# Turning the last state of a gated graph network by DMA instead of by TensorE, with the attention layer one period later

## The chip, the cores and the metric

The kernel runs on one core of a Trainium2 chip. The core has five engines that work through their own instruction queues in order: TensorE (PE, matrix products and transposes), VectorE (DVE), ScalarE (ACT), GpSimd (POOL) and SyncE (SP, which here only issues transfers). Sixteen DMA engines move data. The metric is device time in microseconds (us) of one execution; less is better.

## The reference, cut to what matters

There are 64 graphs of 256 nodes with 256 features each. Two layers follow each other, each on a normalized input and added to `x`:

```python
# layer 0: three steps of a gated graph network
h = jnp.maximum(_layernorm(x, axis=-1), 0.0)
A = (adj != 0).astype(x.dtype)
for i in range(3):
    m = jnp.einsum('bnd,de->bne', h, weight[i])
    aggr = jnp.einsum('bst,bsd->btd', A, m)
    h = _gru_cell(aggr, h, w_ih, w_hh, b_ih, b_hh)   # gates r, z, n from aggr and h; h = (1-z)*n + z*h
x = x + h
# layer 1: graph attention with 4 heads of 64 features
h = jnp.maximum(_layernorm(x, axis=-1), 0.0)
h = (h @ W.T + b).reshape(Bb, Nn, Hh, Cc)
l_src = jnp.einsum('bihc,hc->bih', h, a_src)
l_dst = jnp.einsum('bjhc,hc->bjh', h, a_dst)
logits = jax.nn.leaky_relu(l_src[:, :, None, :] + l_dst[:, None, :, :], ALPHA)
logits = jnp.where(adj_matrix[..., None] == 1, logits, NEG_INF)
probs = jax.nn.softmax(logits, axis=2)
x = x + jnp.einsum('bijh,bjhc->bihc', probs, h).reshape(Bb, Nn, Hh * Cc)
```

## The kernel before, in words

**Tiling.** Two graphs are worked on together, a "pair"; there are 32 pairs, 0 to 31. A tile "by nodes" has nodes on the 128 partitions (`x`, `xn`, `hNhi`, `hNlo`); a tile "by features" has features there (`hT_a`, the state of layer 0; `hT_b`, the normalized input of layer 1). Gates want the state by features, the aggregation over edges and the residual want it by nodes, so the state is turned after each of the three steps.

**The written-out order.** Nothing is scheduled by a tool. `at(tick, phase, p, fn)` puts a piece of work into a plan, and at the end all pieces are emitted tick by tick, in a tick first phase STEP, then READY, then REST, within a phase the later pair first. This one order fixes the queue of every engine. A step of layer 0 takes 6 ticks (`tick_0` to `tick_5`), a pair has its three steps at ticks 0, 12 and 24 after its own start `t0`, and `t0` is 18 ticks after the one of the pair before; so two pairs alternate every 6 ticks, and the order repeats every 18 ticks, called a period here. A tick named alone is counted from a pair's `t0`; "tick 13 of the period" is the same modulo 18.

**Layer 0.** Of a step the later sections name these instructions: `tick_0` builds `pa`, the aggregation (L470), from `hNhi` and `hNlo`; `tick_1` ends with the VectorE sums `T<-aggr,hT_a` and `T<-T,hT_a` (L491, L492); `tick_3` has `pe<-pd,m` on VectorE (L510), which reads the bank `pd` before `tick_4` adds the product `pd<-T,w_h` to it; `tick_4` and `tick_5` have `pn` on VectorE (L526) and TensorE; `new_n` has `R` on GpSimd (L541); `update` writes the new state into `hT_a` (L557 to L559).

**Turning.** `back(l, i)` turns the state of graph `i` by four TensorE transposes into the bank `pback` (L808). After steps 0 and 1 ScalarE and VectorE split it into `hNhi` and `hNlo` for the next aggregation (L798, L799); after step 2 `residual` adds it to `x` on VectorE (L814), at ticks 31 and 32. There are two other ways to turn in the kernel. `plan_turn` does it by way of DRAM: VectorE splits the 32-bit words into 16-bit halves (`halve`, tile `words`, L387), SP stores them (L389), a transposing transfer brings them back (`turn`, tile `turned`, L393), and VectorE puts the halves together (`join`, L399). It serves the normalized inputs, `hT_a` of pairs from 2 on and `hT_b` of pairs up to 28. `plan_relu_T` does it with eight TensorE transposes and two ScalarE instructions for the other pairs (L372, L373).

**Layer 1** of a pair runs between steps of later pairs: normalization at ticks 32 to 34, `values` (`pv`, L864), the score rows by way of DRAM, head maxima (`any`, L949), two accumulating transfers from POOL (L930) that add rows to the logits, `leaky` and `exps` on ScalarE (L969, L984), and `output`: products `po` (L573), `rden` and `o` on VectorE (L582, L584), the addition to `x` on GpSimd (L589), and the store (L562). The adjacency is loaded twice (L115): once for `edge` (L764), once for `noedge` (L838, function `bar`), which is also turned by a transposing transfer into `link` (L916). The last three pairs end in an order of their own (`plan_tail`).

**Buffers.** A tag has as many buffers as `BUFS` says, otherwise one. Tags that the change touches: `x` (5), `adj` (2), `xn` (2), `words` (1), `turned` (1), `hT_a` (2).

## Time and profile before

| | |
|---|---|
| median of 3 runs | 2498.57 us (2495.76 to 2505.38) |
| profiled execution, its own time | 2498.09 us |
| its span, first to last instruction | 2496.3 us |
| granted TensorE clock | 0.997 |
| PE, PEld busy | 99%, 88% |
| DVE, ACT, POOL busy | 80%, 58%, 20% |
| DMA: software queue (POOL), hardware queue (SP) | 27.4%, 27.0% of 16 engines |
| moved | 313.72 MB, mean 126 GB/s |

The page is of one profiled execution. PE is TensorE's products, PEld its weight loads, which overlap them. Products are pipelined: each is shown from its start to its end, and the next starts before that end. The chain of waits follows the work that ended last back to the start. A group of instructions is one line of the kernel with its tiles, with its busy time, the mean duration of one, and the idle time of the engine just before it. The timeline lists one engine's instructions by start (in us from the span's start) and duration; idle time before an instruction stands in brackets, with what ended it.

### The profile page before, as it was taken

The page shows a single profiled execution, that of the slowest core. Times are in us where ns is not written, and L with a number is a line of the kernel's source. Part 1 is how long each engine was busy: PE and PEld are TensorE (multiplying, and loading weights), DVE is VectorE, ACT ScalarE, POOL GpSimd, SP SyncE. Part 2 cuts the span into 40 slices and gives each one's busy share as a digit, 9 for nine tenths or more (in the row PEclk, how much of TensorE's full clock was granted, in tenths as well). Part 3 has the DMA queues.
Part 4 walks back from the last instruction along what each step waited for, and adds up shares of the span by engine and source line. Part 5 has one row for each costly group of instructions (what it writes and reads, how often), then busy time and mean ns, then how long its engine had stood idle before and what let it go on. Part 6 is the DMA issues. An engine that isn't in the chain of part 4 may idle for free.

```text
span 2496.3 us, 37566 instructions
## 1 busy us (share of the span) xinstructions
PE 2464.2 (99%) x13446; PEld 2191.9 (88%) x13446; DVE 1992.2 (80%) x4671; ACT 1437.5 (58%) x3007; POOL 494.3 (20%) x419
## 2 busy tenths in 40 slices
PE   8999999999999999999999999999999999999998
PEld 6888888888988888988888988888888889888887
DVE  5678877888877888777888778888778888778767
ACT  3445556555556555566565566565565555665664
POOL 0011121221221121212121212121212222212212
PEclk9999999999999999999999999999999999999999
DMA  3025656455656456656556565556565556564455
GB/s 95 9 68 119 152 119 153 121 127 134 136 127 155 119 126 143 132 131 147 116 131 148 117 146 138 116 130 147 122 153 127 123 132 140 125 157 118 107 109 110
DMA packets 322090, 313.72 MB, mean 126 GB/s; under 512 B 166560, under 2 KB 282224, under 8 KB 321904
## 3 DMA queue, kind: packets, MB, share of 16 engines
q0 software_dynamic: 33728, 130.03, 27.4%
q1 hardware_dynamic: 286608, 181.29, 27.0%
q8 instruction: 106, 1.74, 0.3%
q14 instruction: 80, 0.66, 0.1%
q10 hardware_dynamic: 1568, 0.01, 0.0%
HBM read 215.62 MB, written 56.60 MB: 109 GB/s over the span
## 4 chain that ended last, share of the span: by engine, by line
PE 83%; DVE 12%; ACT 3%; issue 1%; DMA 1%; POOL 0%; SPq 0%; ACTq 0%; DVEq 0%; POOLq 0%
PE pd L313 18%; PE pn L313 13%; PE pc L313 9%; PE po L573 8%; PE pe L313 7%; PE pa L470 5%; PE qb L448 5%; PE p L313 5%; PE pv L864 5%; PE qa L448 4%; PE pback L808 2%; DVE hT_a L559 2%; DVE any L949 2%; DVE R L558 2%; DVE hNlo L799 1%
## 5 line engine op out<-in xcount | busy, mean ns | idle before, releaser
L313 PE MATMUL pn<-aggr,w_a 128*128 128x256 f32 x1536 | 364.9, 380 | 2.8 <-DVE pn L526 2.8
L313 PE MATMUL pd<-T,w_a 128*128 128x256 f32 x1536 | 366.4, 382 | 0.0
L541 POOL TENSOR_TENSOR R<-hT_a,hn 128x512 f32<-128x512 f32 x96 | 141.9, 1479 | 1124.5 <-ACT hn L537 1042.5
L313 PEld LDWEIGHTS pn<-aggr,w_a 128*128 128x128 f32 x1536 | 286.9, 190 | 44.3 <-DVE pn L526 2.1
L313 PEld LDWEIGHTS pd<-T,w_a 128*128 128x128 f32 x1536 | 288.1, 191 | 37.6
L573 PEld LDWEIGHTS po<-val,zz 128*128 128x128 f32 x2048 | 244.9, 192 | 4.5
L537 ACT ACTIVATE hn<-pn,bi 128x256 f32<-128x256 f32 x384 | 160.4, 470 | 145.6 <-PE pn L313 145.4
L589 POOL TENSOR_TENSOR x<-x,o 128x256 f32<-128x256 f32 x124 | 137.1, 1107 | 538.3 <-DVE o L584 538.3
L558 DVE SCALAR_TENSOR_TENSOR R<-Z,R 128x512 f32<-128x512 f32 x192 | 132.5, 690 | 137.9 <-POOL R L541 126.3
L573 PE MATMUL po<-val,zz 128*128 128x65 f32 x2048 | 242.1, 272 | 0.0
L969 ACT ACTIVATE zz<-zz,val 128x256 f32<-128x256 f32 x496 | 223.7, 505 | 0.0
L949 DVE CUSTOM_DVE_ANT_0 any<-drow,noedge 128x256 f32<-128x256 f32 x496 | 209.1, 422 | 9.3 <-DMA drow<-score_dram 0.5
L455 ACT ACTIVATE R<-pc,brz 128x256 f32<-128x256 f32 x192 | 80.5, 470 | 230.8 <-PE pc L313 230.8
L526 DVE SCALAR_TENSOR_TENSOR pn<-R,hn 128x512 f32<-128x512 f32 x192 | 149.1, 777 | 77.3 <-ACT R L455 54.7
L455 ACT ACTIVATE R<-pe,brz 128x256 f32<-128x256 f32 x192 | 80.4, 470 | 213.5 <-PE pe L313 213.5
L313 PE MATMUL pd<-T,w_h 128*128 128x256 f32 x768 | 184.4, 383 | 3.1 <-DVE pe L510 0.4
L313 PE MATMUL pc<-aggr,w_a 128*128 128x256 f32 x768 | 182.5, 381 | 0.0
L313 PE MATMUL p<-T,w_a 128*128 128x256 f32 x768 | 181.9, 379 | 0.6 <-DVE w_a L247 0.6
L313 PE MATMUL pe<-aggr,w_a 128*128 128x256 f32 x768 | 181.4, 379 | 0.0
L313 PE MATMUL pc<-hT_a,w_h 128*128 128x256 f32 x768 | 181.4, 379 | 0.0
L799 DVE TENSOR_TENSOR hNlo<-pback,hNhi 128x512 fp32r<-128x512 f32 x128 | 88.2, 689 | 110.9 <-ACT hNhi L798 110.9
L313 PEld LDWEIGHTS pd<-T,w_h 128*128 128x128 f32 x768 | 143.5, 190 | 32.8 <-DVE pe L510 14.5
(183 smaller groups left out, 5323.0 us busy)
## 6 DMA issues: line engine op xcount, KB each, us to landing
zz<-score_dram POOLq DMA_DIRECT2D x62, 1024.0 KB, 11.0
zz<-topT_dram POOLq DMA_DIRECT2D x62, 1024.0 KB, 7.9
adj<-in_adj_dram SPq DMA_DIRECT2D x64, 512.0 KB
drow<-score_dram SPq DMA_DIRECT2D x62, 512.0 KB
x<-in_x_dram SPq DMA_DIRECT2D x32, 512.0 KB
out_dram<-x SPq DMA_DIRECT2D x31, 512.0 KB
words_dram_a<-words_a SPq DMA_DIRECT2D x30, 512.0 KB
words_dram_b<-words_b SPq DMA_DIRECT2D x29, 512.0 KB
```

What stands on the lines that cost most here:

```text
L313: nc.tensor.matmul(pt[:, ts(c, N)], w[:, k, j * D + c * P : j * D + (c + 1) * P], src[:, k, :], start=start and c == 0 and k == 0, stop=(c ...
L448: nc.tensor.matmul(pt, w_n[:, j, :], src, start=start, stop=True, skip_group_check=True)
L455: nc.scalar.activation(of(dst, i)[:, c, :], src[:, c, :], AF.Tanh, bias=brz[:, g0 + c : g0 + c + 1], scale=0.5)
L470: nc.tensor.matmul(pt[:, ts(i, N)], hN[half][:, i * KN + s, ts(e, P)], edge[:, i * KN + s, :], start=(s == 0 and half == 0), stop=(s == KN ...
L526: nc.vector.scalar_tensor_tensor(by_c(self.bank(f"pn{i}")), of(self.R, i), 1.0, of(self.hn, i), op0=ALU.add, op1=ALU.mult)
L537: nc.scalar.activation(n__[:, c, :], p_n[:, c, :], AF.Tanh, bias=bi[:, 2 * KD + c : 2 * KD + c + 1])
L541: nc.gpsimd.tensor_sub(of(self.R, i), of(self.hT(), i), n__)
L558: nc.vector.scalar_tensor_tensor(d_, of(self.Z, i), 1.0, d_, op0=ALU.add, op1=ALU.mult)
L573: nc.tensor.matmul(po[:, ts(h_, VC)], zz[:, j, h_, ts(s, P)], v["val"][:, i * KN + j, ts(h_, VC)], start=(j == 0), stop=(j == KN - 1),)
L589: add(v["x"][:, r, :], v["x"][:, r, :], o)
L949: nc.vector.tensor_tensor_reduce(any_, drow[r // KN][:, h, :], v["noedge"][:, r, :], 1.0, -3.0e38, ALU.add, ALU.max, accum_out=v["top"][:, ...
L969: nc.scalar.activation(zz[:, h, :], zz[:, h, :], AF.Prelu, alpha=ALPHA, bias=v["val"][:, r, S0 + H + h : S0 + H + h + 1],)
```

## The change

For pairs 0 to 21 ("home") the state after the third step is turned by `plan_turn`: halved at tick 31, turned at tick 33, joined at tick 37 into a buffer of tag `xn`, and then added to `x` by an accumulating transfer from POOL at tick 38. The TensorE transposes and the two additions on VectorE of that step are not emitted for them. Layer 1 of a pair starts `S` ticks later: 18 for home pairs, 15, 12, 9, 6 and 3 for pairs 22 to 26, and 0 from pair 27 on. Pairs 22 to 26 turn their normalized input with `plan_relu_T` instead of `plan_turn`. `adj` has one buffer instead of two, and its two loads and the making of `noedge` are moved (first load to tick -5; second load to tick 40 for home pairs and `bar` to tick 46, from 22 and 35); `x` has six buffers instead of five. The second turning transfer of home pairs (`turned_b`) is issued at tick 37 + 18 instead of 35, and `link` at 38 + 18 instead of 37. `plan_turn` is written for any shape of blocks.

```diff
--- before.py
+++ after.py
@@ -99,7 +99,7 @@
         return ps_m.tile([P, 512], F32, tag="mm", name=name)
 
     BUFS = {
-        "x": 5, "adj": 2, "edge": 2, "noedge": 2, "hT_a": 2, "xn": 2, "val": 2, "row": 2, "zz": 4, "o": 2,
+        "x": 6, "adj": 1, "edge": 2, "noedge": 2, "hT_a": 2, "xn": 2, "val": 2, "row": 2, "zz": 4, "o": 2,
     }
 
     def buf(tag, shape, name, dtype=F32):
@@ -377,27 +377,30 @@
             at(t, REST, p, fn(k))
         return w
 
-    def plan_turn(src, tag, name, p, ticks):
+    def plan_turn(src, dst, name, p, ticks):
+
 
 
         w = {}
 
         def halve():
-            words = buf("words", [P, R, 2, D], f"words_{name}", U16)
-            nc.vector.tensor_copy(words, src().bitcast(U16).rearrange("q r (d w) -> q r w d", w=2))
-            w["rows"] = dram.tile([R, P, 2 * D], U16, tag="words", name=f"words_dram_{name}")
-            nc.sync.dma_start(w["rows"].rearrange("r q e -> q r e"), words.rearrange("q r w d -> q r (w d)"))
+            y = src()
+            nb, n = y.shape[1:]
+            words = buf("words", [P, nb, 2, n], f"words_{name}", U16)
+            nc.vector.tensor_copy(words, y.bitcast(U16).rearrange("q b (n w) -> q b w n", w=2))
+            w["rows"] = dram.tile([nb, P, 2 * n], U16, tag="words", name=f"words_dram_{name}")
+            nc.sync.dma_start(w["rows"].rearrange("b q e -> q b e"), words.rearrange("q b w n -> q b (w n)"))
 
         def turn():
-            w["turned"] = buf("turned", [P, 2, KD * T], f"turned_{name}", U16)
-            nc.sync.dma_start_transpose(
-                w["turned"].rearrange("q w (k n) -> q (w k) n", k=KD), w["rows"].rearrange("r q e -> (r q) e")
-            )
+            nb, _, n2 = w["rows"].shape
+            w["turned"] = buf("turned", [P, n2 // P, nb * P], f"turned_{name}", U16)
+            nc.sync.dma_start_transpose(w["turned"], w["rows"].rearrange("b q e -> (b q) e"))
 
         def join():
-            w["hT"] = buf(tag, [P, KD, T], f"hT_{name}")
+            w["hT"] = dst()
             nc.vector.tensor_copy(
-                flat(w["hT"]).bitcast(U16).rearrange("q (n w) -> q n w", w=2), w["turned"].rearrange("q w n -> q n w")
+                flat(w["hT"]).bitcast(U16).rearrange("q (n w) -> q n w", w=2),
+                flat(w["turned"]).rearrange("q (w n) -> q n w", w=2),
             )
 
         at(ticks[0], READY, p, halve)
@@ -757,7 +760,8 @@
         if p == 0:
             v["x"], v["adj"] = first
         else:
-            rest(-16, lambda: v.update(x=load_x(p), adj=load_adj(p, "adj")))
+            rest(-16, lambda: v.update(x=load_x(p)))
+            rest(-5, lambda: v.update(adj=load_adj(p, "adj")))
 
         def to_edge():
             v["edge"] = buf("edge", [P, R, N], f"edge_{p}", F32R)
@@ -770,7 +774,9 @@
         ready(-1 if p else -2.5, to_edge)
         if dma_a:
             ready(-9.5, lambda: nc.scalar.activation(flat(xn_a["xn"]), flat(xn_a["xn"]), AF.Relu))
-            h = plan_turn(lambda: xn_a["xn"], "hT_a", f"a{p}", p, [t0 - 9, t0 - 8, t0 - 3])
+            h = plan_turn(
+                lambda: xn_a["xn"], lambda: buf("hT_a", [P, KD, T], f"hT_a{p}"), f"a{p}", p, [t0 - 9, t0 - 8, t0 - 3]
+            )
         else:
             h = plan_relu_T(xn_a, "hT_a", f"a{p}", p, [t0 - 4, t0 - 3])
 
@@ -812,6 +818,16 @@
         def residual(i):
             xi = flat(v["x"][:, i * KN : (i + 1) * KN, :])
             nc.vector.tensor_add(xi, v["pback", i], xi)
+
+
+
+        S = max(0, min(3 * SUB, 3 * (NPAIR - 5 - p)))
+        home = S == 3 * SUB
+        if home:
+            h_3 = plan_turn(
+                lambda: h["hT"], lambda: buf("xn", [P, R, D], f"h_{p}"), f"h{p}", p, [t0 + 31, t0 + 33, t0 + 37]
+            )
+            rest(38, lambda: nc.gpsimd.dma_start(flat(v["x"]), flat(h_3["hT"]), accum_op=ALU.add))
 
         for l in range(L):
             end = last and l == L - 1
@@ -826,7 +842,8 @@
                 ready(t + SUB, lambda g=g: g.update(0))
                 ready(t + SUB, lambda g=g: g.update(1))
                 for i in range(PB):
-                    rest(t + SUB + 1 + i, back(l, i))
+                    if not (home and l == L - 1):
+                        rest(t + SUB + 1 + i, back(l, i))
 
 
         def load_adj_1():
@@ -840,19 +857,23 @@
                 v["noedge_rows"] = dram.tile([R, P, N], BF16, tag="noedge", name=f"noedge_dram_{p}")
                 nc.sync.dma_start(v["noedge_rows"].rearrange("r q t -> q r t"), v["noedge"])
 
-        rest(16 if last else 22, load_adj_1)
-        ready(28 if last else 35, bar)
+
+        rest(16 if last else 22 + S if S > 12 else 36 if S >= SUB else 22, load_adj_1)
+        ready(28 + S if S > 12 else 40 if S >= SUB else 30 if S else 28, bar)
         if last:
             plan_tail(t0, p, v, g, lambda i: turn_back(L - 1, i), residual)
             return
 
-        dma_b = p < NPAIR - 3
-        later = SUB if dma_b else 0
-        xn_b = plan_norm(lambda: v["x"], f"b{p}", p, [t0 + 32, t0 + 33, t0 + 33, t0 + 34], dma_b)
+        dma_b = S in (0, 3 * SUB) and p < NPAIR - 3
+        later = SUB + S if p < NPAIR - 3 else 0
+        xn_b = plan_norm(lambda: v["x"], f"b{p}", p, [t0 + S + t for t in (32, 33, 33, 34)], dma_b)
         if dma_b:
-            hb = plan_turn(lambda: xn_b["xn"], "hT_b", f"b{p}", p, [t0 + 34.1, t0 + 35, t0 + 41])
+            hb = plan_turn(
+                lambda: xn_b["xn"], lambda: buf("hT_b", [P, KD, T], f"hT_b{p}"), f"b{p}", p,
+                [t0 + S + t for t in (34.1, 37 if home else 35, 41)],
+            )
         else:
-            hb = plan_relu_T(xn_b, "hT_b", f"b{p}", p, [t0 + 35, t0 + 36])
+            hb = plan_relu_T(xn_b, "hT_b", f"b{p}", p, [t0 + S + 35, t0 + S + 36])
 
         def values(r0):
             def fn():
@@ -932,7 +953,7 @@
                 )
             return fn
 
-        rest(37 if dma_b else 36, linked)
+        rest(38 + S if home else 37 + S if p < NPAIR - 3 else 36, linked)
         ready(38 + later, barred_in(0, 0))
         ready(39 + later, barred_in(0, 1))
         ready(40 + later, barred_in(1, 0))

```

## The prediction

> **What bounds the kernel now.** I read the page's engine row first, then the groups, then the transposes by their tile name, and then one period in order of time, engine by engine. First the page:

> ```profile
> PE 2464.2 (99%) x13446; PEld 2191.9 (88%) x13446; DVE 1992.2 (80%) x4671; ACT 1437.5 (58%) x3007; POOL 494.3 (20%) x419
> ...
> PE 83%; DVE 12%; ACT 3%; issue 1%; DMA 1%; POOL 0%; SPq 0%; ACTq 0%; DVEq 0%; POOLq 0%
> ...
> L313 PEld LDWEIGHTS pd<-T,w_h 128*128 128x128 f32 x768 | 143.5, 190 | 32.8 <-DVE pe L510 14.5
> ```

> TensorE is the bound: 99% busy, 83% of the last chain. It runs from product to product, so what counts is the distance between starts. First `pa` products 18 ticks apart lie 75.48 us apart in nearly every period from tick 78 to tick 546. The third line is the one regular hole: `pd<-T,w_h` waits for VectorE's `pe` (L510). The work to be removed, by its tile:

> ```profile
> L808 PE MATMUL pback<-ident,hT_a x768: 272/273/417, 52.4 to 2454.0; 128*128 128x128 f32 x192
> ...
> L814 DVE TENSOR_TENSOR x<-pback,x x64: 658/687/692, 138.5 to 2455.0; 128x512 f32<-128x512 f32 x64
> ```

> Now one period in order of time (start, duration, then the instruction; brackets are idle time before it). VectorE's queue:

> ```profile
> 1275.06 0.18 DVE L582 RECIPROCAL rden<-po 128x4 f32<-128x4 f32 x1 [0.39 <-PE po L573]
> ...
> 1280.91 0.68 DVE L838 TENSOR_SCALAR noedge<-adj 128x1024 bf16<-128x1024 int32 x1
> ...
> 1282.32 0.18 DVE L582 RECIPROCAL rden<-po 128x4 f32<-128x4 f32 x1
> ...
> 1288.61 0.69 DVE L492 TENSOR_TENSOR T<-T,hT_a 128x512 f32<-128x512 f32 x1
> ...
> 1293.52 0.69 DVE L799 TENSOR_TENSOR hNlo<-pback,hNhi 128x512 fp32r<-128x512 f32 x1 [0.54 <-ACT hNhi L798]
> 1294.13 0.69 DVE L510 TENSOR_TENSOR pe<-pd,m 128x512 f32<-128x512 f32 x1
> ```

> and TensorE's:

> ```profile
> 1258.75 0.60 PE L808 MATMUL pback<-ident,hT_a 128*128 128x128 f32 x4
> 1259.19 1.89 PE L313 MATMUL p<-T,w_a 128*128 128x256 f32 x8
> ...
> 1280.10 1.90 PE L573 MATMUL po<-val,zz 128*128 128x65 f32 x16
> ...
> 1294.17 0.59 PE L448 MATMUL qb<-T4n,w_n 128*128 128x256 f32 x2
> 1294.87 1.99 PE L313 MATMUL pd<-T,w_h 128*128 128x256 f32 x8
> ```

> Four transposes take 0.44 us of TensorE's order (1258.75 to 1259.19), though each shows 0.273. `qb` pairs elsewhere are followed 0.43 later, so `pd` could start at 1294.60 and starts at 1294.87: a hole of 0.27 us. VectorE has one idle gap of 0.39 between 1262.5 and 1293, and reaches the `rden` at 1282.32 only 0.3 after its `po` ended (1282.00). From there to `pe` it has no slack of its own: the 0.54 before `hNlo` comes round by ScalarE from VectorE's own `hn`.

> [...] here f32 transposes go by every 0.109 us. [...] a 1 MB accumulate lands in a median 11.0 us beside other transfers, 7.9 elsewhere.

> **The change part by part**, against the profiled execution (2498.09 us, span 2496.3, 1.8 around it; 0.5 below the median 2498.57).

> *Transposes removed.* S is 18 for pairs 0 to 21 ("home"): 22 x 8 x 0.109 = -19.2 us on the bound engine.

> *Transposes added.* Pairs 22 to 26 (S = 15, 12, 9, 6, 3) turn the normalized x on TensorE again: 5 x 8 x 0.109 = +4.4. Net -14.8.

> *VectorE, ticks 13 to 17.* Two residual adds go (0.60 of its queue each), `words_h` comes (1.14, the rate of `words_a`, 1243.30 to 1244.43). It stands before the wait for `qb` at 1261.98, where VectorE idled 1.30: hidden. Without that cover it costs 0.5 a period.

> *noedge* goes from tick 17 to tick 10, into a stretch idle 3.1 us at 1249.9: free there. At tick 17 it frees 0.60 of queue, but only 0.3 counts, as `rden` then waits for `po`.

> *join of h* (1.15, as `hT_a` at 1266.61 to 1267.76) comes right after `T<-T,hT_a` at 1288.61, in the stretch without slack. From `po`'s end: `rden` 0.03 later, 11.81 from `rden` to `pe` as shown (1282.32 to 1294.13), +1.15, and 0.74 from `pe`'s start to `pd`'s: 13.73. TensorE needs 1294.60 - 1282.00 = 12.60. The hole becomes 1.13, +0.86. It needs the head maxima beside it, which start with tick 67 of pair 0; so joins of pairs 2 to 21: 20 x 0.86 = +17.2. Bounds: 0 if something else absorbs it, 1.15 + 0.3 a period if the freed 0.3 doesn't come: 0 to +24.

> *Periods without a join.* The 0.27 hole is seen 29 times; it stays inside the 20 above, and the nine others lose it at most: -2.4.

> *Catch-up.* Layer 1 of pairs 22 to 27 follows at 15 ticks instead of 18. Counting queue times, VectorE holds 22 to 26 us for each six ticks there, against 24 to 28 for TensorE; the regular worst six ticks hold 29.4 against 25.7 and pass with 0.27. But xn of S = 3 and the statistics of S = 6 fall in ticks 1 to 4, without slack. I take 3; bounds 0 and +20 (4 for each of five pairs).

> *Layer 1 a period later*: the same products later; ticks 24 to 42, without layer 1, already run at 64.3 us for 18, its work. Nothing.

> *Transfers.* Each home pair adds a store, a transpose and an accumulate of 512 KB, on SP, SP and POOL. SP now has `words_h` store, adj load and `turned_h` behind `turned_a`; DMA is idle from 1267 to 1277 and the join comes at 1289: hidden. `turned_b` then waits for the join (the one `turned` buffer), and out of turn behind it in SP's queue stand x, link and adj. The old places of those:

> ```profile
> 1206.62 3.16 SPq L393 DMA_TRANSPOSE turned_b<-words_dram_b  x1
> ...
> 1213.43 0.39 SPq L120 DMA_DIRECT2D x<-in_x_dram  x1
> ```

> After: join over at 1214.7 on this period's clock, `turned_b` issued in 2 to 3 us, x at 1217 to 1218. Its data, with the accumulate interleaved, is through at 1221.5 to 1224. `st_a` reads x at 1222.26, then 0.9 later than that because of the hole; `pn` behind it waits for ScalarE anyway and is due on TensorE at 1226.5: lateness up to some 1.8 us costs nothing. Link (read from tick 8), adj (tick 10) and `hT_b` (1225.89) have 5 us or more. POOL waits for the join too; behind it stands `R` at 1226.37, after an idle 17.6. The sixth x buffer keeps the reuse distance of before; the one adj buffer alternates with 3 ticks or more to spare. Free.

> Sum: -19.2 + 4.4 + 17.2 - 2.4 + 3 = +3.0; 2498.1 + 3.0 = **2501 us**.

> **Rivals.** *The join is absorbed.* Then -14.8 and the holes as before or gone: 2481 to 2486. For it: 1.3 and 3.1 us idle elsewhere on VectorE; against: none between 1282 and 1293. *The late x.* If x lands later than 1.8 us after `st_a` wants it, every further microsecond is one of TensorE, 20 times: at +1.5 us that is +30, with the sum 2531. It decides from a landing at about 1225. For it: SP's queue is in order and the transpose's issue takes up to 3.4 us; against: four microseconds of idle DMA from 1220. *Catch-up in VectorE's tight ticks*, 3 to 4 us for each of five pairs: 2513 to 2518. *The transfers are only hidden work* and the hole is 0.5 instead of 0.86: 2494.

> **How the numbers follow.** Cancelling, with smaller and larger holes: 0.53 (2488 to 2510). Join absorbed: 0.13. Late x: 0.15. Catch-up: 0.19. A change under 0.5% (12.5 us) can't be told from none here. Faster 0.13 (the absorbed join alone), slower 0.34 (the late x and the catch-up), same 0.53. The range leaves out the fastest absorbed cases and the late x from 1.2 us on: 2484 to 2524.

> **What would show it.** `pback` down to 592; a hole of about 1.1 us before `pd<-T,w_h` once a period, laid to `pe`, in the periods from tick 72 to 430; the period there still 75.5 us; the two before it under 65. A period of 74.6 says the join is absorbed. A wait of `st_a` for x, or of `hT_b` for `turned_b`, says transfers are late. Periods over 80 between ticks 440 and 545 say catch-up. I am wrong if VectorE's queue in ticks 17 to 21 has a slack that this one period hides, or if DMA beside the accumulate is slower than these windows.

## The result and the profile after

The changed kernel takes 2530.8 us (median of 4 runs, 2523.8 to 2532.3); the kernel before took 2502.0 on the same chip at the same time. The ratio is 1.0112, with a 95% interval of 1.0081 to 1.0144: slower, by about 28 us. The forecast was 2501 with a range up to 2524. The profiled execution is the quickest of the four: 2523.8 us, span 2522.0, 25.7 above the span of before.

First the page of the kernel after: the engine row, the row of the last chain, and two groups of products (busy us, mean ns of one, then the idle time just before them and what ended it).

```profile
PE 2455.3 (97%) x13310; PEld 2182.0 (87%) x13310; DVE 2012.7 (80%) x4661; ACT 1442.4 (57%) x3017; POOL 514.1 (20%) x441
...
PE 80%; DVE 14%; ACT 3%; DMA 2%; issue 1%; POOL 0%; SPq 0%; DVEq 0%; POOLq 0%; ACTq 0%
...
L313 PE MATMUL pn<-aggr,w_a 128*128 128x256 f32 x1536 | 367.8, 383 | 13.0 <-DVE pn L529 13.0
...
L313 PE MATMUL pd<-T,w_h 128*128 128x256 f32 x768 | 184.1, 383 | 22.3 <-DVE pe L513 22.3
```

TensorE has less to do (2455 us busy, 2464 before) and yet ends later: it is idle. Two groups wait: `pd<-T,w_h` for `pe`, as forecast (3.1 before), and `pn<-aggr,w_a` for `pn` on VectorE, which was not forecast (2.8 before).

The transposes by tile name, and the regular period in order of time: VectorE's queue first, then TensorE's (start, duration, instruction, idle time before it in brackets).

```profile
L814 PE MATMUL pback<-ident,hT_a x592: 272/273/328, 52.3 to 2479.0; 128*128 128x128 f32 x198
```

```profile
1273.69 0.69 DVE L495 TENSOR_TENSOR T<-T,hT_a 128x512 f32<-128x512 f32 x1
1274.29 1.22 DVE L401 COPY h<-turned_h 128x2048 uint16<-128x2048 uint16 x1
...
1280.34 0.69 DVE L513 TENSOR_TENSOR pe<-pd,m 128x512 f32<-128x512 f32 x1
```

```profile
1279.54 0.59 PE L451 MATMUL qb<-T4n,w_n 128*128 128x256 f32 x2
1281.08 1.99 PE L313 MATMUL pd<-T,w_h 128*128 128x256 f32 x8 [0.95 <-DVE pe L513]
```

`pback` fell from 768 to 592, which is 22 x 8 fewer. The join of h stands where it was expected, and `pd` starts 1281.08 - 1279.54 - 0.43 = 1.11 us after it could: the forecast was 1.13. So the regular period is as forecast, 75.45 us against 75.48. The time went elsewhere. The stretch view of the kernel after, one row for each stretch of 18 ticks: the first is a regular period, the others start at ticks 420, 438, 456, 474, 492, 510 and 528. Columns: stretch, length, busy time (and instructions) of PE, PEld, DVE, ACT and POOL, granted clock (the share of full speed that TensorE got), DMA share, GB/s.

```profile
762.00:837.45 75.45, 74.50 (x407) 66.57 (x405) 62.86 (x145) 44.41 (x94) 17.05 (x16) 1.00 0.76 154
1742.88:1818.13 75.25, 75.25 (x415) 67.34 (x413) 61.83 (x145) 44.52 (x94) 15.91 (x14) 1.00 0.57 134
1818.13:1898.31 80.18, 79.96 (x438) 71.22 (x437) 62.33 (x148) 47.41 (x99) 16.88 (x15) 1.00 0.50 116
1898.31:1980.17 81.86, 77.09 (x423) 67.65 (x422) 63.19 (x149) 49.23 (x102) 12.39 (x11) 1.00 0.50 123
1980.17:2064.03 83.86, 79.18 (x427) 69.58 (x425) 65.60 (x162) 47.57 (x99) 22.46 (x20) 0.98 0.64 135
2064.03:2143.74 79.71, 78.64 (x442) 70.26 (x441) 61.07 (x153) 48.56 (x99) 15.05 (x13) 1.00 0.71 119
2143.74:2231.68 87.94, 84.41 (x462) 75.18 (x461) 66.55 (x163) 49.28 (x101) 19.64 (x16) 0.96 0.63 140
2231.68:2311.37 79.69, 76.00 (x416) 67.03 (x414) 63.28 (x151) 45.59 (x96) 15.71 (x14) 1.00 0.57 133
```

The six periods from tick 438 on are the catch-up, in which layer 1 comes back from 18 ticks late to none. They take 493.2 us. The work that belongs there comes to 468.3: six periods as before (6 x 75.48 = 452.9), 4.4 for the added transposes, and 11.0 for the layer 1 of one pair that was put off from the start. (A period without layer 1 takes 63.37 us at its steadiest, one with it and without a hole 74.37, as `e7_join_43` below shows.) **The catch-up thus loses 24.9 us**, where the forecast had 3, and that is nearly the whole difference in this execution. The granted clock is below 1 in two of the six.

What such a loss is made of, in the kernel after at 1916 to 1923 us. Three queues in order of time: VectorE, GpSimd, TensorE.

```profile
1916.19 0.69 DVE L529 SCALAR_TENSOR_TENSOR pn<-R,hn 128x512 f32<-128x512 f32 x1
1916.80 0.68 DVE L523 TENSOR_TENSOR Z<-pd,m 128x512 f32<-128x512 f32 x1
1917.80 2.06 DVE L353 TENSOR_SCALAR xn_b<-x,mv_b,rstd_b 128x256 f32<-128x256 f32 x4 [0.33 <-POOL rstd_b L348]
...
1920.24 1.55 DVE L970 CUSTOM_DVE_ANT_0 any<-drow,noedge 128x256 f32<-128x256 f32 x1
...
1921.72 0.69 DVE L529 SCALAR_TENSOR_TENSOR pn<-R,hn 128x512 f32<-128x512 f32 x1
```

```profile
1917.74 1.23 POOL L951 DMA_DIRECT2D zz<-topT_dram  x1
1918.50 1.70 POOL L951 DMA_DIRECT2D zz<-score_dram  x1
1920.02 1.48 POOL L544 TENSOR_TENSOR R<-hT_a,hn 128x512 f32<-128x512 f32 x1
```

```profile
1917.03 1.97 PE L313 MATMUL pn<-aggr,w_a 128*128 128x256 f32 x8 [0.65 <-DVE pn L529]
1918.83 1.89 PE L313 MATMUL pd<-T,w_a 128*128 128x256 f32 x8
1922.47 1.99 PE L313 MATMUL pn<-aggr,w_a 128*128 128x256 f32 x8 [1.74 <-DVE pn L529]
```

TensorE has only `pd` between its two `pn` products. In that time VectorE makes the normalized input of layer 1 (`xn_b`) and head maxima (`any`), the second of which takes 1.55 us beside GpSimd's `R` instead of the usual 0.42. VectorE works in order (its second `pn` starts at 1921.72, just as `any` ends), so this `pn` comes late and TensorE stands (1.74 us). (This `pn` reads the half of `R` that ScalarE made by 1917.3; GpSimd's `R` is the other graph's, so it is not what `pn` waits for.) Such a stretched `any` stands five times in this trace: of 512, five take 0.95 to 1.55 us, and each of these starts while GpSimd's `R` (four times) or `x<-x,o` (once) runs and ends 0.28 to 0.29 us after it, here at 1921.79 against 1921.50. The other 507 take 0.39 to 0.43 us. Why `any` is held up is not shown.

### The profile page after: what moved, and what is told of

It reads as the page before. It is cut to its first block, busy times and chain, and to the rows that moved or that the text cites. A ratio compares the mean times of both kernels' runs of the same rounds, so it can differ in the third digit from the quotient of the medians.

```text
span 2522.0 us, 37423 instructions
## 1 busy us (share of the span) xinstructions
PE 2455.3 (97%) x13310; PEld 2182.0 (87%) x13310; DVE 2012.7 (80%) x4661; ACT 1442.4 (57%) x3017; POOL 514.1 (20%) x441
## 4 chain that ended last, share of the span: by engine, by line
PE 80%; DVE 14%; ACT 3%; DMA 2%; issue 1%; POOL 0%; SPq 0%; DVEq 0%; POOLq 0%; ACTq 0%
PE pd L313 17%; PE pn L313 12%; PE pc L313 10%; PE po L576 8%; PE pe L313 6%; PE pa L473 5%; PE qb L451 5%; PE p L313 5%; PE pv L885 4%; PE qa L451 4%; DVE hT_a L562 2%; DVE any L970 2%; PE pback L814 2%; DVE R L561 1%; DVE hNlo L805 1%
## 5 line engine op out<-in xcount | busy, mean ns | idle before, releaser
L313 PE MATMUL pn<-aggr,w_a 128*128 128x256 f32 x1536 | 367.8, 383 | 13.0 <-DVE pn L529 13.0
L313 PE MATMUL pd<-T,w_a 128*128 128x256 f32 x1536 | 366.4, 382 | 0.0
L313 PEld LDWEIGHTS pn<-aggr,w_a 128*128 128x128 f32 x1536 | 287.6, 191 | 58.3 <-DVE pn L529 12.9
L313 PEld LDWEIGHTS pd<-T,w_a 128*128 128x128 f32 x1536 | 288.4, 191 | 37.2
L592 POOL TENSOR_TENSOR x<-x,o 128x256 f32<-128x256 f32 x124 | 131.7, 1063 | 536.0 <-DVE o L587 536.0
L313 PE MATMUL pd<-T,w_h 128*128 128x256 f32 x768 | 184.1, 383 | 22.3 <-DVE pe L513 22.3
L313 PEld LDWEIGHTS pd<-T,w_h 128*128 128x128 f32 x768 | 143.9, 190 | 50.7 <-DVE pe L513 32.3
L313 PE MATMUL p<-T,w_a 128*128 128x256 f32 x768 | 182.0, 380 | 0.6 <-DVE w_a L247 0.6
L313 PE MATMUL pc<-aggr,w_a 128*128 128x256 f32 x768 | 182.5, 381 | 0.0
L313 PE MATMUL pc<-hT_a,w_h 128*128 128x256 f32 x768 | 182.1, 380 | 0.0
L313 PE MATMUL pe<-aggr,w_a 128*128 128x256 f32 x768 | 181.4, 379 | 0.0
```

The costliest lines, as they stand in the source:

```text
L313: nc.tensor.matmul(pt[:, ts(c, N)], w[:, k, j * D + c * P : j * D + (c + 1) * P], src[:, k, :], start=start and c == 0 and k == 0, stop=(c ...
L592: add(v["x"][:, r, :], v["x"][:, r, :], o)
```

## The experiments

The theory after these traces: the catch-up alone loses the time, because layer 1 slides against layer 0 and VectorE's work for it comes into ticks in which TensorE has nothing to fill in. Rivals: the new transfers are at fault, or x is late, or VectorE is simply too full there. All runs are compared with the kernel before on the same chip (2497.9 to 2498.7 us by the median). This table has the regular period and the six periods of the catch-up, taken from the distances of first `pa` products:

| kernel | regular | six periods of the catch-up | sum |
|---|---|---|---|
| after | 75.45 | 80.18, 81.86, 83.86, 79.71, 87.94, 79.69 | 493.2 |
| e1_pe_back | 75.23 | 80.48, 81.87, 83.34, 80.20, 83.66, 79.69 | 489.2 |
| e3_grid6 | 75.45 | 75.24, 85.40, 80.64, 83.03, 83.89, 79.38 | 487.6 |
| e4_x_first | 75.45 | 80.18, 81.86, 83.78, 79.78, 92.37, 79.67 | 497.7 |
| e5_norm_out | 75.45 | 79.74, 78.33, 77.67, 79.72, 84.48, 79.70 | 479.6 |
| e7_join_43 | 74.37 | 80.19, 81.87, 82.41, 82.02, 95.17, 79.68 | 501.3 |
| e8_join_twice | 78.4 | 80.21, 81.85, 83.23, 80.26, 83.05, 79.67 | 488.3 |
| e9_norm_later | 75.45 | 81.38, 78.35, 77.81, 78.85, 83.95, 79.69 | 480.0 |
| e10_link_later | 75.46 | 80.19, 81.86, 83.73, 79.83, 84.40, 79.69 | 489.7 |
| e11_all | 74.37 | 81.37, 78.34, 77.83, 78.84, 83.81, 79.68 | 479.9 |

In `after`, `e4_x_first` and `e8_join_twice` the catch-up is the same piece of program, and it takes 493.2, 497.7 and 488.3 us. So two single executions can differ by some 9 us there for no reason of the program, almost all of it in the fifth of the six periods; a smaller difference between two traces proves nothing by itself.

### e1_pe_back: the later layer 1 without the new turning

```diff
-        home = S == 3 * SUB
+        home = False
```

> The shift and the catch-up alone: layer 1 is a period later and the pairs at the end catch up by 3 ticks each, as in the changed kernel, but the third state is turned on TensorE and added to x on VectorE as before. Theory (the steady periods come out even, and the loss lies in the catch-up): 22 pairs get 8 transposes of 0.109 us back (+19), the hole before pd<-T,w_h falls from 1.13 to 0 to 0.3 in 20 periods (-17 to -22), period about 75.2 us, the catch-up periods still 80 to 88 us; span 2517 to 2524, as slow as the changed kernel. Rival (the new transfers and the accumulate make it slow): the span falls back to about 2500.

Measured: 2524.6 us (ratio 1.010, 1.0082 to 1.0118), span 2515.2. The state is turned by TensorE as before, yet the catch-up loses 489.2 - 468.3 = 20.9 us. The loss belongs to the later layer 1 and the way back from it, not to the transfers. The regular period is 75.23 instead of 75.48: the hole of 0.27 us is gone, as `noedge` left that stretch. Set beside 74.37 in `e7_join_43`, this splits the regular period: 75.23, less 0.87 for the eight transposes, is 74.36, and the rest, 1.08, is the join's.

### e2_join_late: the join out of the tight stretch

```diff
-                ..., f"h{p}", p, [t0 + 31, t0 + 33, t0 + 37]
+                ..., f"h{p}", p, [t0 + 31, t0 + 41, t0 + 45]
...
-            rest(38, lambda: nc.gpsimd.dma_start(flat(v["x"]), ...
+            rest(46, lambda: nc.gpsimd.dma_start(flat(v["x"]), ...
...
-                [t0 + S + t for t in (34.1, 37 if home else 35, 41)],
+                [t0 + S + t for t in (34.1, 35, 41)],
```

> The turn by DRAM of the third state is transposed at tick 41 and joined at tick 45 (added at 46) instead of 33, 37 and 38, where VectorE idled 1 to 3 us; the turning of the normalized input goes back to tick 35. Theory (the join in VectorE's tight stretch makes the hole of 1.13 us): the hole is gone or at most 0.3, the period falls from 75.45 to 74.4 in 20 periods, span 2498 to 2503; the catch-up periods stay at 80 to 88. Rival (the hole has another cause, such as the accumulate or late transfers): period stays at 75.4, span 2520 or more.

Measured: 2838.5 us (ratio 1.134, 1.129 to 1.140), regular periods of 82 to 97 us. Neither theory had this. The view of waits names it (total, times, longest), and the stretches around one such wait show its ground (columns as above):

```profile
DVE hT_a L401 <- DMA turned_a<-words_dram_a: 328.7, 20, 22.8
```

```profile
626.00:632.00 6.00, 6.00 (x36) 5.52 (x35) 4.56 (x8) 4.85 (x10) 3.29 (x3) 1.00 1.07 232
632.00:638.00 6.00, 6.00 (x37) 5.48 (x37) 5.46 (x16) 3.83 (x6) 0.00 (x0) 1.00 1.58 88
```

The transposing transfer `turned_a` is issued from 626.3 to 633.3 us, right beside the accumulating `zz<-score` of 626.9 and 629.5, and is joined only at 657.7. While both are in flight, the DMA engines are reported busier (1.58 instead of 1.07) and move 88 GB/s instead of 232. The waits bring half clock with them: in the slow periods TensorE ran at half speed for 314 us, so some 157 of the 340 us lost are the clock's. On the place of the join the run says nothing.

### e6_no_add: the same without the accumulating transfer to x

```diff
-            rest(46, lambda: nc.gpsimd.dma_start(flat(v["x"]), flat(h_3["hT"]), accum_op=ALU.add))
```

(against `e2_join_late`)

> The kernel with the join at tick 45 and turned_b at tick 35 (e2_join_late), with the accumulating transfer of the state to x left out, so that layer 0's result doesn't reach x for pairs 0 to 21. It tells whether e2 was slow by the collision of the transposing turned_a with the accumulating transfer. If so: turned_a lands within 5 us of its issue again, hT_a doesn't wait for it, and the steady period shows what the place of the join is worth: 74.4 us if the place alone made the hole before pd (hole 0.3 or less), 75.4 if the join costs the same anywhere. If the late join itself made e2 slow, the periods stay over 80.

Measured: a single execution, span 2519.9. The regular period is 74.37 us (74.6 and 76.3 in a few early ones), and `hT_a` waits for `turned_a` 3 times for 5.6 us in all, where it waited 20 times for 328.7. So the late join is harmless, and the period is 1.08 us shorter (that the place of the join brings this, and not the missing transfer, `e7_join_43` shows, which has the transfer); what made `e2_join_late` slow was how its transfers met. The transfer left out is not the one seen beside `turned_a`; without it the others shift. `turned_a` is issued at 632.3, when the accumulate before it has landed (625.7) and 2.6 us before the next, not 0.5; that next one lands 9.6 us after its issue, where it took 33.2 in `e2_join_late`.

### e7_join_43: the join moved, the whole computation

```diff
-                ..., f"h{p}", p, [t0 + 31, t0 + 33, t0 + 37]
+                ..., f"h{p}", p, [t0 + 31, t0 + 41, t0 + 43]
...
-            rest(38, lambda: nc.gpsimd.dma_start(flat(v["x"]), ...
+            rest(45.5, lambda: nc.gpsimd.dma_start(flat(v["x"]), ...
...
-                [t0 + S + t for t in (34.1, 37 if home else 35, 41)],
+                [t0 + S + t for t in (34.1, 35, 41)],
```

> The whole computation, with the state turned at tick 41, joined at tick 43 (the period's tick 7) and added at tick 45.5, turned_b at tick 35. If no transposing transfer falls beside the accumulating one: steady period 74.4 us, the hole before pd gone, catch-up unchanged, span 2498 to 2504. If one does: periods over 80 us as in e2_join_late, with turned_a landing over 15 us after its issue. If the join costs the same at any tick: 75.4 and 2522.

Measured: 2510.0 us by the median of 13 runs (ratio 1.0038, 1.0022 to 1.0053), spread from 2499.6 to 2518.9. The regular period is 74.37 as expected, so the join costs 1.08 us at tick 37 and nothing at tick 43. The span missed: 2508.2 by the median (1.8 under the time) instead of 2498 to 2504, which only four of the 13 runs reached. The profiled execution is the slowest of them, 2517.1. Its catch-up lost 33.0, about half of it in one period of 95.17, and after tick 546 it lost another 7.2 (217.9 us to the end, 210.6 in the kernel after), with 17.07 us at half clock. ScalarE's queue in the period of 95.17, then TensorE's:

```profile
2132.68 1.06 ACT L1005 ACTIVATE zz<-zz 128x1024 f32<-128x1024 f32 x1 [9.30 <-DMA zz<-topT_dram]
2133.65 0.37 ACT L466 COPY qb<-qa 128x256 f32<-128x256 f32 x1
```

```profile
2134.07 1.22 PE L451 MATMUL qa<-T,w_n 128*128 128x256 f32 x2 [7.43 <-ACT qb L466]
```

ScalarE waits 9.30 us for an accumulating transfer, with the `qb` of the next step queued behind, and TensorE stands 7.43 us for that. That transfer was issued at 2103.4 us and had landed at 2132.7, 29 us later, with the transposing `link` issued at 2099.8 in its way. It is the meeting of `e2_join_late` again, now in the catch-up.

### e4_x_first: is x late?

```diff
-                [t0 + S + t for t in (34.1, 37 if home else 35, 41)],
+                [t0 + S + t for t in (34.1, 38 if home else 35, 41)],
```

> The turning transfer of the normalized input is issued one tick later, behind the load of x and not ahead of it, in SP's queue. Theory (VectorE's wait of 0.8 us for x at the statistics lies beside slack): that wait is gone, the period stays at 75.45 and the time within 3 us of the changed kernel. Rival (late x, every microsecond counts): the period falls by about 0.8 us in 20 periods, 15 us in all.

Measured: 2530.6 us (ratio 1.0131, 1.0112 to 1.015), regular period 75.45, unchanged. In the kernel after, `st_a` does wait for x, 21 times and 17.3 us in all; here it waits twice, 6.1 us in all, and the period does not feel it. The view of waits, first of the kernel after, then of this one (total, times, longest):

```profile
DVE st_a L341 <- DMA x<-in_x_dram: 17.3, 21, 3.3
```

```profile
DVE st_a L341 <- DMA x<-in_x_dram: 6.1, 2, 3.2
```

The rival *The late x* is out. This trace shows one thing more. The profiled execution of the kernel after is its quickest, 7 us under its median; the one here takes 2530.1 us, as long as that median. Its catch-up loses 29.4 us, 4.5 more, all in one period: 92.37 us instead of 87.94, with 10.24 us at half clock. `e10_link_later` shows what differs there.

### e3_grid6: a fall in steps of six ticks

```diff
-        S = max(0, min(3 * SUB, 3 * (NPAIR - 5 - p)))
+        S = max(0, min(3 * SUB, SUB * ((NPAIR - 4 - p) // 2)))
```

> The catch-up goes by 6 ticks every second pair (S = 18, 12, 12, 6, 6, 0 for pairs 22 to 27) instead of by 3 ticks every pair, so layer 1 always meets the steps of layer 0 at the same tick of a step; pair 22 is a home pair too. Theory (instructions of layer 1 stand at the wrong tick of a step: VectorE waits in order for pv and is then late for the gates, and each stall of about 2 us brings 3.4 us of half clock): the steady period stays 75.45, the stalls of the catch-up fall from 25 us to under 10, no half clock there, span 2502 to 2510. Rival (the catch-up costs because more work falls into each period, wherever it stands): span 2515 to 2525.

Measured: 2520.0 us (ratio 1.0091, 1.0076 to 1.0107); the catch-up loses some 20 us. The span of 2517.5 lies in the range of its rival, more work in each period wherever it stands, which `e9_norm_later` then puts aside. (As to the theory's half clock: in the kernel after the stalls of 2.26, 1.59 and 1.94 us at 2057.58, 2146.00 and 2197.53 us were each followed by 3.41 us of it, the one of 1.74 us at 1920.72 was not.) It was not the tick within a step that mattered. What the steps of three and of six have in common is the other partner: in the regular order the normalization of pair p (ticks 50 to 52 of p) stands beside the `po` products of pair p-2 (its ticks 86 to 89, which are 50 to 53 of p). Where S falls from pair to pair, `po` of p-2 comes 6 ticks after the normalization (3 for pair 22). TensorE then lacks its filling and reaches `pd` and `pn` before VectorE does. The next two runs test this.

### e5_norm_out: the normalization taken away

```diff
+        if 0 < S < 3 * SUB:
+            xn_b = {}
+            at(t0 + S + 34, READY, p, lambda: xn_b.update(xn=v["x"]))
+        else:
             xn_b = plan_norm(lambda: v["x"], f"b{p}", p, [t0 + S + t for t in (32, 33, 33, 34)], dma_b)
```

> The changed kernel, but for pairs 22 to 26 (the ones that catch up) the normalization of layer 1's input is left out: neither statistics nor scaling of x on VectorE and ScalarE, x itself is turned. Products, transposes and the rest stay. Theory (VectorE is loaded in ticks where TensorE has filling products less, and is late with pn and pe): the stalls of TensorE between 1910 and 2290 us fall from 25 us to 10 or less, the periods from tick 440 on to 77 to 80, no stretch at half clock there, span 2507 to 2512 us. Rival (the order of products and ScalarE's part set the stalls, VectorE's load does not): stalls stay near 20 us, span 2516 to 2522. The steady period stays 75.45 under both.

Measured: 2510.7 us (ratio 1.0055, 1.0034 to 1.0076), span 2508.8. The catch-up loses 11.3 instead of 24.9 us. The single periods are within the expected 77 to 80 except the one at 84.48, and one half-clock stretch stayed. The normalization (on VectorE 4.5 us for each of five pairs: 1990.4 us busy instead of 2012.7; a small part on GpSimd, `rstd_b`, is gone with it) carries a good half of the loss. The run cannot tell whether VectorE has too much to do, or only at the wrong time.

### e9_norm_later: the same normalization six ticks later

```diff
-        xn_b = plan_norm(..., [t0 + S + t for t in (32, 33, 33, 34)], dma_b)
+        xn_b = plan_norm(..., [t0 + S + t + (6 if 0 < S < 18 else 0) for t in (32, 33, 33, 34)], dma_b)
...
-            hb = plan_relu_T(xn_b, "hT_b", f"b{p}", p, [t0 + S + 35, t0 + S + 36])
+            hb = plan_relu_T(xn_b, "hT_b", f"b{p}", p, [t0 + S + t + (6 if 0 < S < 18 else 0) for t in (35, 36)])
```

> The whole computation; for pairs 22 to 26 the normalization of layer 1's input and its transposes come six ticks later, so that they fall beside the po products of two pairs before, as they do in the regular period. Theory (the same VectorE work hurts only where TensorE has no filling products beside it): the six periods from tick 438 on, 493.2 us together in the changed kernel, fall to 478 to 485, stalls from 25 to 10 to 16 us, span 2508 to 2514 us. Rival (VectorE is simply too full in the catch-up, wherever its work is put): 490 us or more, span 2519 or more.

Measured: 2511.8 us (ratio 1.0061, 1.0046 to 1.0076), span 2509.5; the catch-up takes 480.0 us and loses 11.7. Moving the work gains as much as leaving it out: it was in the wrong ticks, and VectorE is not too full. (The transposes of that input moved with it; in `e5_norm_out` they stayed and the gain was the same, so it is not theirs. Of the 13.2 us gained on the kernel after, 4.0 are in the fifth period, which varies by itself; the medians, 2530.8 and 2511.8, are clear of each other.) TensorE's queue where the new place stands, and VectorE's beside it:

```profile
1939.96 1.89 PE L313 MATMUL pe<-aggr,w_a 128*128 128x256 f32 x8
1941.69 1.90 PE L576 MATMUL po<-val,zz 128*128 128x65 f32 x16
1943.42 1.95 PE L313 MATMUL pn<-aggr,w_a 128*128 128x256 f32 x8
```

```profile
1940.13 0.70 DVE L529 SCALAR_TENSOR_TENSOR pn<-R,hn 128x512 f32<-128x512 f32 x1
...
1941.34 1.37 DVE L353 TENSOR_SCALAR xn_b<-x,mv_b,rstd_b 128x256 f32<-128x256 f32 x4
```

`xn_b` runs beside a `po` that gives VectorE 1.73 us, and the `pn` after it starts without a wait.

### e10_link_later: one transposing transfer out of the way

```diff
-        rest(38 + S if home else 37 + S if p < NPAIR - 3 else 36, linked)
+        rest(38 + S if home else 45.5 if p == NPAIR - 6 else 37 + S if p < NPAIR - 3 else 36, linked)
```

> The changed kernel with one transfer moved: link of pair 26 (a transposing transfer) is queued at tick 45.5 instead of 40, behind words_a of pair 29. In the changed kernel it is issued at 2121.4 us, between two accumulating transfers, and the second of these lands 21 us after its issue instead of 6 to 9; ScalarE waits 3.5 us for it with the qb of the next step behind. If that collision costs: the accumulating transfer lands within 14 us, the period at 2144 us falls from 87.9 to 80 to 83 us, span 2514 to 2518 us. If it doesn't: that period stays over 86 us, span 2522.

The ground for it, two stretches of the kernel after, in which `link` meets the accumulating `zz<-topT` (over the whole of that execution the accumulates to `zz` land 7.7 to 29.6 us after their issue, 9.5 by the median):

```profile
2125.00:2130.00 5.00, 5.00 (x31) 4.52 (x29) 4.97 (x12) 2.06 (x4) 3.78 (x4) 1.00 1.12 178
2130.00:2141.00 11.00, 11.00 (x54) 9.69 (x54) 10.25 (x34) 8.20 (x17) 0.87 (x1) 1.00 1.43 41
```

Again the DMA share rises and the rate falls, to 41 GB/s. Measured with `link` moved: the second transfer lands 9.4 us after its issue instead of 21.1 (2126.0 to 2135.4), ScalarE no longer waits for it, and the period falls from 87.94 to 84.40. So the wait is the collision's; the fall of the period, 3.5 us, is less than the 5 to 8 expected. The median is 2519.7 (ratio 1.0086, 1.0071 to 1.0101, which still touches the interval of the changed kernel); the profiled span of 2519.1 is a little over the expected 2514 to 2518, those of the three other runs are 2515.8 to 2518.9.

What the collision costs differs from execution to execution. In seven traces `link` of pair 26 stands at its old place with this part of the program unchanged. The landing of that second transfer (us after its issue) and the period from tick 510:

| kernel | landing | period |
|---|---|---|
| e10_link_later (`link` moved) | 9.4 | 84.40 |
| e8_join_twice | 12.7 | 83.05 |
| e1_pe_back | 15.0 | 83.66 |
| after | 21.1 | 87.94 |
| e4_x_first | 24.3 | 92.37 |
| e2_join_late | 25.5 | 93.91 |
| e6_no_add | 26.2 | 94.96 |
| e7_join_43 | 29.3 | 95.17 |

With landings of 9.4 to 15.0 us the period is 83.05 to 84.40; with landings of 21.1 to 29.3 it is 87.94 to 95.17, up to 11 us more than with `link` moved, half clock included. Why one execution meets longer than another is not known.

### e8_join_twice: what a longer hole costs

```diff
-            nc.vector.tensor_copy(
+            for _ in range(2 if name[0] == "h" else 1):
+                nc.vector.tensor_copy(
```

> The join of h done twice for pairs 0 to 21, all else as in the changed kernel. If VectorE has no slack between rden and pe, each further 1.15 us there is one of TensorE: hole before pd 1.12 to 2.3 us, steady period 76.6, span 2542 to 2548 us. If part of it is absorbed: period under 76.1.

Measured: a single execution, 2573.6 us, span 2571.8 instead of 2542 to 2548. The hole is as expected: 0.26 us before `qb` and 2.05 before `pd`, 2.31 in all. (Of the 2.05 the trace marks 1.88 as idle, of the 1.11 in the kernel after 0.95, since products overlap.) But only two of the regular periods take the expected 76.7; the others take 78.4. One such hole, and one period of each kind in the stretch view:

```profile
378.14 1.99 PE L313 MATMUL pd<-T,w_h 128*128 128x256 f32 x8 [1.88 <-DVE pe L514]
```

```profile
310.52:387.23 76.71, 74.73 (x406) 66.41 (x405) 63.91 (x146) 44.31 (x94) 16.81 (x15) 1.00 0.66 152
387.23:465.63 78.40, 76.43 (x407) 67.56 (x405) 64.10 (x146) 44.32 (x94) 16.80 (x15) 0.98 0.67 148
```

The same instructions take 1.7 us more at a granted clock of 0.98. Of 20 holes of 2.0 us, 16 are followed by a stretch of 3.41 us at half speed that starts within 1.5 us of the hole's end, which loses 1.7 us. (One period reached 78.6 by another wait instead.) The 19 holes of 1.11 us in the kernel after started none.

### e11_all: the mends together

Moved join (`e7_join_43`), later normalization (`e9_norm_later`) and later `link` (`e10_link_later`), each by the diff above.

> The join at tick 43 (e7_join_43) with both mends of the catch-up. By the sum: steady period 74.37 us, the catch-up some 480 us for six periods, span 2484 to 2494 us, 2486 to 2496 by the median, thus 2 to 12 us under the kernel before. If the mends don't add to the moved join: 2499 to 2510 as e7_join_43.

Measured: 2490.3 us by the median of 7 runs (2489.8 to 2491.5), before 2497.9: ratio 0.9971, 0.9959 to 0.9982. It beats the kernel before by 7.6 us, less than the 12.5 that the prediction took for the least to be told from none, yet with an interval clear of 1; and the changed kernel, each set against the kernel before on its own chip, by some 35. The page of this kernel:

```profile
PE 2447.8 (98%) x13310; PEld 2177.1 (87%) x13310; DVE 2008.4 (81%) x4661; ACT 1442.5 (58%) x3017; POOL 511.2 (21%) x441
...
L313 PE MATMUL pn<-aggr,w_a 128*128 128x256 f32 x1536 | 365.6, 381 | 8.4 <-DVE pn L529 8.4
...
L313 PE MATMUL pd<-T,w_h 128*128 128x256 f32 x768 | 184.1, 382 | 2.7 <-DVE pe L513 2.7
```

The idle time before `pd` is down from 22.3 to 2.7 us and the one before `pn` from 13.0 to 8.4. The 11.6 us still lost in the catch-up were not pursued.

## Why the prediction was wrong

**The step that failed is *Catch-up*.** It had +3 us, with bounds 0 and +20; measured are 24.9 in the quickest execution, outside even the bounds. All other steps sum to 0.0 in the forecast (-19.2 + 4.4 + 17.2 - 2.4), and 25.7 was measured for the whole, so they were right within a microsecond together. Three things were wrong in that one step:

- It compared VectorE's queue time with TensorE's over six ticks at a time (22 to 26 us against 24 to 28) and took the regular worst six ticks, 29.4 against 25.7, as proof that more would pass. Those pass because `po` stands in the very ticks where the normalization is; the balance over six ticks doesn't see that. It looked for tight ticks only at S = 3 and 6; the stall shown at 1922 us stands at tick 460, where the normalization of pair 23 is, with S = 12. `e9_norm_later` shows it: the same work six ticks later saves 13.2 us.
- It moved instructions in time and not transfers. `link` of pair 26 came between two accumulating transfers, and in the kernel before no transposing transfer moves its data beside an accumulating one for more than 0.3 us. The price is 3.5 us in the trace of the kernel after (87.94 against 84.40 in `e10_link_later`), 8.0 in the one of `e4_x_first`, 10.8 in `e7_join_43`; these are differences of single executions.
- It had no term for the clock and so counted a stall at its own length. In the profiled execution three stalls of the catch-up were followed by 3.41 us at half clock, some 5.1 us in all.

The second and third overlap with each other and with the first, so the parts don't add up to 24.9.

**The other points.** *Transposes removed* and *added*: right, 592 are left. *join of h*: right, hole 1.11 for 1.13 forecast, and it is the join that makes it, as the period of 74.37 with the join elsewhere shows. *noedge*: right, `e1_pe_back` shows the hole of 0.27 closed by it. *Layer 1 a period later*: right, two early periods fell to 63.4 and the 11.0 us put off come back at the end; its price is in the way back, not in the delay. *Transfers* free: right for x (`e4_x_first`), and for the regular period as it is written, but not a property of the transfers: with `turned_h` at tick 41 instead of 33, `turned_a` was caught by the accumulates and the kernel took 340 us more.

**The rivals.** *Catch-up in VectorE's tight ticks* was the right one, with the right sign of it ("periods over 80 between ticks 440 and 545": four of the six are), priced at 2513 to 2518 and given 0.19; it deserved the larger part. *The join is absorbed* is false at tick 37, and true at tick 43.

## What to carry to other kernels

Where two pipelines of work slide against each other, don't weigh the queues over a stage: for each late instruction on the second engine ask which filling work the bound engine had beside it in the old phase, and where that filling is in the new one. When a shift loses time, move the auxiliary work by the same shift before giving it up; here six ticks regained half of the loss. List transposing and accumulating transfers in one order of time whenever either kind moves.

## What the runs showed of the hardware

```profile
2058.00:2060.20 2.20, 0.36 (x2) 0.34 (x3) 2.13 (x7) 0.46 (x2) 0.40 (x1) 1.00 1.07 213
2060.20:2064.00 3.80, 3.80 (x13) 3.11 (x12) 2.98 (x11) 0.98 (x3) 2.27 (x2) 0.55 1.03 206
```

The clock is 1.00 while TensorE stands (0.36 of 2.20 us busy) and falls when it is at work again: 0.55 in the view's next stretch (3.80 of 3.80 us busy).

**A transposing transfer beside an accumulating one** stretched both where they met for long: 88 GB/s for 232 in `e2_join_late`, 41 for 178 in the kernel after, a landing of the accumulate in 21 to 29 us for 9.4. The packets in the traces (256 bytes for a transposing transfer, 4096 for an accumulating one) show it over all transfers of 512 KB: in the kernel before, none of the 59 transposing ones moves beside an accumulating one for more than 0.3 us, and they take 2.2 to 4.5 us from first packet to last; in `e2_join_late` 20 of 76 do so for 11 us or more and take 14.4 to 31.2 us, while the 55 that do so for under 1 us take 2.1 to 3.9. A meeting of 1 to 2 us often passed cheaply (3.0 to 5.9 us). With under 1 us of an accumulating one beside it, none took over 4.5 us in these two traces. Why the pair is slow, and whether the size of the pieces matters, stays open.
